# A graph layer on one core: TensorE waits for the gathered rows by a small product, one-hots in pairs, two more groups taken by hand

## The chip, the core and the metric

The kernel runs on one core of a Trainium2 chip. A core has TensorE (PE in the profile; PEld is its loading of weights), VectorE (DVE), ScalarE (ACT), GpSimd (POOL) and SyncE (SP), each with a queue of its own that it works through in order; instructions of different queues are ordered by semaphores. DMA queues are fed by SyncE and GpSimd. The metric is the device time of one launch in microseconds, here the median of three runs.

## The reference, cut to what matters

x has 12,500 nodes of 128 features; there are 400,000 edges, sorted by their destination, each with 32 features of its own.

```python
h = relu(layernorm(x))
m = relu(concat(h[src], h[dst], edge_attr) @ w1 + b1) @ w2 + b2      # per edge
agg = segment_sum(m, dst, num_segments=12500)                        # per node
gi, gh = agg @ w_ih + b_ih, h @ w_hh + b_hh                          # a GRU cell
r, z = sigmoid(gi_r + gh_r), sigmoid(gi_z + gh_z)
n = tanh(gi_n + r * gh_n)
return x + (1 - z) * n + z * h
```

## The kernel before, in words

**Once per node.** The setup normalises x, keeps h transposed in SBUF (`hT_all`), and writes A = h @ w1[0:128] to memory, a row of 128 floats for each node. B = h @ w1[128:256] + b1 is made batch by batch. The product with w2 is moved behind the sum over edges, so an edge needs only relu(A[src] + B[dst] + edge_attr @ w1[256:288]).

**Groups.** The edges are cut into 3125 tiles of 128 and these into NP = 391 groups of 8 tiles (the first has 5). A group's destinations fall into two windows of 32 nodes. For group k and its two halves (units u = 2k and 2k + 1) this is done:

- The rows A[src] are fetched into a buffer `G[k]` (128 edges by 8 tiles by 128 features). As a rule GpSimd does it, by 8 indirect DMAs, one for each tile (`gather`, line 156). There are 11 buffers. The first nine groups (RAW) fetch rows of x instead, and normalise and multiply them.
- `pre` (L673): TensorE multiplies the matrix `L` (one-hots of the destinations and the edges' features, made by VectorE at L575) with `RW` (the window's rows of B, and w1's last rows) into PSUM.
- `add` (L701): in the unit of the second half VectorE adds `G[k]` to the product and takes the relu, for the whole group in one instruction, into one of two buffers `RB`.
- `onehot` (L623): VectorE compares the destinations (`dloc`) with a row of 0 to 31 and writes eight 128 by 32 one-hots into one of six buffers `OH`. The row of numbers lies in columns 256 to 287 of both PSUM banks of sums (`SEGB`); the bank is read that is not open at the time.
- `seg` (L719, L724): TensorE multiplies RB with the one-hots and sums in one of the two banks, which is used for two groups (k // 2 picks it). A product of zeros (L719) opens a bank. `take` (L733) copies the sums of two groups out, in the last quarter of the unit after.

**Groups by hand.** GpSimd doesn't fetch for all groups. 27 are taken by VectorE and 28 by ScalarE, which copy the columns of `hT_all` that the 1024 sources name into `HE` (L960 on ScalarE, one column each; L967 on VectorE, two columns packed into one instruction, and a copy L972 after 128 columns); the numbers are loaded into registers at L945, 16 at a time on ScalarE and 32 on VectorE. TensorE then multiplies `HE` by w1a (L684), adding to the same PSUM, and ScalarE takes the relu (L710) instead of VectorE's add. Two groups are fetched by SyncE, row by row. `SPREAD` says how many groups each takes; they are spread evenly over the 391, and each engine's jobs follow each other without a break: `run_jobs` gives a job's steps out over the four quarters of its units.

**Order.** Everything is written out in Python and compiled in that order; nothing reorders it. In unit u the loop calls `gathers` (asks for the gathers whose buffer is free by program order), a quarter of the hand steps, then `stages(u)`: one-hots for group u // 2 + 3 (odd u), `pre` for unit u + 3, `add` for unit u + 2; then two more quarters of hand steps, `seg(u)`, and in the last quarter `take` and a step of the node work. The node work (`node`, a GRU cell for 512 nodes, some 14 groups each) is cut into steps of one unit.

**Waits.** The framework sets a wait wherever an instruction needs what another engine or a DMA has done, also where TensorE writes into a PSUM bank that another engine reads, whatever the columns. An instruction holds one wait; more stand in event-semaphore instructions of two waits each ahead of it on the same queue. So an `add` of a gathered group has four event semaphores ahead of it, for the eight gathers (each has a semaphore of eight that take turns) and one for TensorE.

Of the kernel before, what the change touches and what calls it, by code (L numbers as in the profile page):

```python
# [9 lines left out]
F32 = mybir.dt.float32  # L10
# [19 lines left out]
V = 32  # L30
# [14 lines left out]
RAW = 9  # L45
# [7 lines left out]
PIECE = 128  # L53
STEP = {"act": 4, "dve": 8, "sp": 4}
ROW = 4 * D
SPREAD = {"dve": 27, "act": 28, "sp": 2}
START = {"dve": 14, "act": 4, "sp": 24}
NR = 12672

# [4 lines left out]
def tile_gnn(ctx: ExitStack, tc: tile.TileContext, x, src, srcT, dstT, dstP, eaT, eaP, w1, b1, w2T, b2,  # L64
             wih, bih, whh, bhh, out):
    nc = tc.nc
    ctx.enter_context(tc.manual_schedule())
    const = ctx.enter_context(tc.tile_pool(name="const", bufs=1))
# [12 lines left out]
    def tiles(k):  # L81
        return (0 if k == 0 else SUP0 + (k - 1) * PAIR, SUP0 + k * PAIR)
# [57 lines left out]
    G = {}  # L140
# [7 lines left out]
    def gather(k):  # L148
        if k >= NP or k in mode:
            return  # L150
        G[k] = gp.tile([128, GRP, 2, D], F32, name="G")
        table = x if k < RAW else A
        for u in (2 * k, 2 * k + 1):
            for t, j, a in unit_tiles(u):
                c, i = divmod(t, CH)
                nc.gpsimd.indirect_dma_start(  # L156
                    out=G[k][:, j, a, :], out_offset=None, in_=table,
                    in_offset=bass.IndirectOffsetOnAxis(ap=src_i[c][:, i:i + 1], axis=0))

    for k in range(RAW):  # L160
        gather(k)
# [2 lines left out]
    RB = [const.tile([128, PAIR, D + 4], F32, name=f"RB{i}") for i in range(2)]  # L164
    for r in RB:
        nc.vector.memset(r[:, :, D:], 1.0)
    OHB = [const.tile([128, GRP, 2, V], F32, name=f"OH{i}") for i in range(6)]
    nc.vector.memset(OHB[0], 0.0)


# [433 lines left out]
                                  "(p f) -> p f", p=V))  # L604

    def onehot(k):
        if k >= NP:
            return
        t0, t1 = tiles(k)
        OH[k] = OHB[k % len(OHB)]  # L610
        row = SEGB[((k - 3) // 2 + 1) % 2][:, 256:256 + V]
        for a in range(2) if k == 0 else (None,):
            if a is None:
                o, s = OH[k].rearrange("p j a v -> p a j v"), slice(t0, t1)
                d = dloc[:, s].rearrange("p (a j) -> p a j", a=2)[:, :, :, None]
                shape = [128, 2, GRP, V]
                i = row[:, None, None, :]
            else:
                e = min(t1, (a + 1) * GRP)
                o, d = OH[k][:, :e - a * GRP, a, :], dloc[:, a * GRP:e, None]  # L620
                shape = [128, e - a * GRP, V]
                i = row[:, None, :]
            nc.vector.tensor_tensor(o, d.to_broadcast(shape), i.to_broadcast(shape),  # L623
                                    op=ALU.is_equal)

    def unit(u):
        k, h = divmod(u, 2)
# [59 lines left out]
    def add(u):  # L687
# [15 lines left out]
        if h == 1:  # L703
            PP.pop(k)
            G.pop(k, None)

    def relu(u):
        if u in RT:
            o, p = RT.pop(u)
            nc.scalar.activation(o, p, AF.Relu)  # L710
# [4 lines left out]
    def seg(u):  # L715
        k, h = divmod(u, 2)
        p = SEGB[(k // 2) % 2]
        if h == 0 and k % 2 == 0:
            nc.tensor.matmul(p[:, :D + 1], zrow[:, :128], zrow[:, :D + 1], start=True, stop=False)  # L719
        l = unit_tiles(u)  # L720
        rest = l if h else l + unit_tiles(u + 1)
        for i, (t, j, a) in enumerate(l):
            r0 = 2 * V * (k % 2) + V * a
            nc.tensor.matmul(p[r0:r0 + V, :D + 1], OH[k][:, j, a, :],  # L724
                             RB[k % 2][:, 2 * j + a, :D + 1], start=False,
                             stop=all(b != a for _, _, b in rest[i + 1:]))

# [206 lines left out]
    def one_by_one(m, k):  # L934
# [8 lines left out]
        for e0 in range(0, PAIR * 128, LOAD[m]):  # L943
# [4 lines left out]
            if m == "sp":  # L948
                for i, v in enumerate(vals):
                    e = e0 + i  # L950
                    a, j = divmod(e // 128, GRP)
                    nc.sync.dma_start(rows[e % 128:e % 128 + 1, j, a, :],
                                      A_bytes[bass.ds(v, ROW)].rearrange("(o f) -> o f", o=1))
                    if i % STEP[m] == STEP[m] - 1:
                        yield
                continue
# [64 lines left out]
    def stages(u):  # L1021
        if u + 7 >= 0:
            raw_stats(u + 7)
        if u + 6 >= 0:
            raw_fin(u + 6)
            raw_h(u + 6)
        if u % 2 == 0:
            onehot_T(u // 2 + 3)
        elif u > -7:
            onehot(u // 2 + 3)  # L1030
        if u + 4 >= 0:
            raw_turn(u + 4)
        if u + 3 >= 0:
            pre(u + 3)
        if u + 2 >= 0:
            add(u + 2)
            relu(u + 2)
# [232 lines left out]
```

## Time and profile before

| | us |
|---|---|
| median of three runs (3400.22 to 3402.1) | 3400.61 |
| the profiled execution | 3403.76 |
| its span, first to last instruction | 3401.8 |
| TensorE busy | 2417.4 (71%) |
| VectorE busy | 2225.1 (65%) |
| ScalarE busy | 3079.4 (91%) |
| GpSimd busy | 2566.1 (75%) |
| mean granted clock of TensorE | 0.796 |

A row by source line reads: line, engine, operation, what it writes from what it reads, shape, count, then the busy time and the mean of one in ns, then the engine's idle time just before these instructions and what ended most of it. Where two instructions overlap on an engine, the mean is longer than busy time by count. "Issue" as the end of idle time means that the profile shows nothing that was waited for: register loads, event semaphores and dispatch are the sequencer's and not counted as busy. A row of the waits reads: who waited, for whom, total, times, longest. A row of the timeline: start, duration, engine, line and operation, count, and in brackets the idle time before it. A row of the windows: the stretch and its length, then for PE, PEld, DVE, ACT and POOL the busy time with the number of instructions, the granted clock, and the DMA engines' share and GB/s. A row of one source line gives the shortest, median and longest duration in ns and the first and last start; a q behind the engine means its sequencer.

### The profile page before, as it was taken

Reading aid. Unit: us, or ns where it says so; the run is one execution under the profiler, and the core shown is the slowest. Engines: PE = TensorE matmul, PEld = TensorE weight load, DVE = VectorE, ACT = ScalarE, POOL = GpSimd, SP = SyncE. Lnnn points to the kernel's source line nnn. Section 1 sums busy time; section 2 is a strip of 40 time slices with the busy share of each in tenths; the row PEclk is TensorE's granted clock in tenths of the full one; section 3 lists DMA queues with packets and bytes.
Section 4 is the critical chain, followed back from the end, with each engine's and each line's share of the span. In section 5 each row is a group of like instructions: output and inputs, shape, how many; then the busy total and the mean of one; then the engine's idle time right before and its main releaser. Section 6 shows DMA issues by size and latency. Waiting matters only on the chain. (4 is left out here: it accounts for less than half of the span.)

```text
span 3401.8 us, 88642 instructions
## 1 busy us (share of the span) xinstructions
PE 2417.4 (71%) x13113; PEld 1563.7 (46%) x13113; DVE 2225.1 (65%) x16468; ACT 3079.4 (91%) x29057; POOL 2566.1 (75%) x2678
## 2 busy tenths in 40 slices
PE   7567777777677767776777667676677767766767
PEld 7444444444445444544444444444444434444445
DVE  8556666666676666666666666666666666666665
ACT  7699999999999998999899988988988898898984
POOL 7777777777777777777777777777777777777776
PEclk9777887887887778777877877788777778777878
DMA  6434444434443333343434433443433334343332
GB/s 213 106 88 93 97 100 99 101 94 100 102 98 94 98 99 95 95 101 97 98 93 99 98 94 93 96 96 93 98 93 92 95 94 99 92 97 96 92 92 73
DMA packets 191316, 335.44 MB, mean 99 GB/s; under 512 B 66753, under 2 KB 112384, under 8 KB 190729
## 3 DMA queue, kind: packets, MB, share of 16 engines
q0 software_dynamic: 85408, 175.09, 23.0%
q1 hardware_dynamic: 105177, 154.58, 16.4%
q14 instruction: 478, 3.92, 0.4%
q8 instruction: 109, 1.79, 0.2%
q10 hardware_dynamic: 144, 0.07, 0.0%
HBM read 309.24 MB, written 20.24 MB: 97 GB/s over the span
## 5 line engine op out<-in xcount | busy, mean ns | idle before, releaser
L156 POOL DMA_INDIRECT G<-A,src_i x2600 | 2498.9, 961 | 796.2 <-issue 753.7
L960 ACT COPY HE_act<-hT_all 128x4 uint8 x28672 | 2886.8, 189 | 51.4 <-issue 27.0
L967 DVE SCALAR_TENSOR_TENSOR both<-hT_all 128x4 uint16 x13824 | 1173.4, 153 | 988.5 <-issue 980.7
L673 PE MATMUL pre<-RW,L 128*128 128x256 f32 x3128 | 1132.4, 488 | 229.8 <-DVE RB L701 220.6
L673 PEld LDWEIGHTS pre<-RW,L 128*128 128x128 f32 x3128 | 660.6, 236 | 506.1 <-DVE RB L701 234.0
L724 PE MATMUL seg<-RB,OH 128*32 128x129 f32 x6250 | 603.9, 324 | 380.0 <-DVE RB L701 349.7
L724 PEld LDWEIGHTS seg<-RB,OH 128*32 128x32 f32 x6250 | 333.1, 125 | 820.4 <-DVE RB L701 532.7
L701 DVE CUSTOM_DVE_ANT_0 RB<-pre,G 128x1024 f32<-128x1024 f32 (+1 forms) x326 | 394.5, 1210 | 62.7 <-DMA G<-A,src_i 49.2
L575 DVE TENSOR_SCALAR L<-L,node_of 64x512 f32<-64x512 int32 x382 | 186.7, 489 | 9.7 <-DMA L<-in_dstP 9.4
L719 PE MATMUL seg<-zrow 1*128 1x129 bf16 x196 | 45.3, 231 | 164.4 <-DVE OH L623 164.2
L623 DVE TENSOR_TENSOR OH<-dloc,seg 128x256 f32<-128x256 f16 (+1 forms) x392 | 159.5, 407 | 0.5 <-issue 0.5
L750 PE MATMUL nd<-spot,sums 128*128 128x40 f32 x782 | 116.6, 321 | 1.2 <-DVE sums L733 1.2
L750 PEld LDWEIGHTS nd<-spot,sums 128*128 128x128 f32 x782 | 112.4, 231 | 10.5 <-issue 9.0
L710 ACT ACTIVATE RB<-pre 128x1024 f32<-128x1024 f32 x64 | 65.0, 1015 | 52.4 <-PE pre L684 52.4
L809 ACT ACTIVATE gt<-nd 128x512 f32<-128x512 f32 (+2 forms) x28 | 16.4, 585 | 96.5 <-PE nd L803 96.5
L972 DVE COPY HE_dve<-both 128x512 uint8<-128x512 uint8 x216 | 96.6, 447 | 7.4
L684 PEld LDWEIGHTS pre<-w1a,HE_act 128*128 128x128 f32 x448 | 88.4, 245 | 11.6
L684 PEld LDWEIGHTS pre<-w1a,HE_dve 128*128 128x128 f32 x432 | 87.9, 252 | 12.1
L684 PE MATMUL pre<-w1a,HE_act 128*128 128x128 f32 x448 | 86.4, 327 | 0.0
L684 PE MATMUL pre<-w1a,HE_dve 128*128 128x128 f32 x432 | 85.1, 333 | 0.0
L156 POOL DMA_INDIRECT G<-in_x,src_i x69 | 65.9, 954 | 21.8 <-issue 20.7
L233 PE MATMUL nd<-w1b,hT_all 128*128 128x128 f32 x224 | 45.5, 346 | 43.3 <-DVE xb L835 43.3
(177 smaller groups left out, 1383.9 us busy)
## 6 DMA issues: line engine op xcount, KB each, us to landing
L<-in_dstP SPq DMA_DIRECT2D x195, 256.0 KB
L<-in_eaP SPq DMA_DIRECT2D x195, 256.0 KB
G<-A,src_i POOLq DMA_INDIRECT x2600
G_sp<-A SPq DMA_DIRECT2D x2048, 0.5 KB
RW<-B SPq DMA_DIRECT2D x782, 16.0 KB
xb<-in_x SPq DMA_DIRECT2D x26, 256.0 KB
out<-xb SPq DMA_DIRECT2D x26, 256.0 KB
xs<-in_x SPq DMA_DIRECT2D x11, 512.0 KB
```

Of the source, the lines that this page charges most:

```text
L156: nc.gpsimd.indirect_dma_start(out=G[k][:, j, a, :], out_offset=None, in_=table, in_offset=bass.IndirectOffsetOnAxis(ap=src_i[c][:, i:i + ...
L575: nc.vector.tensor_scalar(o, i, node_of[:, k:k + 1], None, op0=ALU.is_equal)
L623: nc.vector.tensor_tensor(o, d.to_broadcast(shape), i.to_broadcast(shape), op=ALU.is_equal)
L673: nc.tensor.matmul(p[:, 2 * i:2 * i + 2, :], Ls[k // QP][:, c0:c0 + 128], RW[k % 4], start=True, stop=not raw)
L684: nc.tensor.matmul(p[:, 2 * i + a, :], cols, w1a, start=False, stop=n + 1 == len(l) or l[n + 1][1] != j)
L701: nc.vector._custom_dve(TENSOR_ADD_SAT, out=o, in0=p, in1=G[k].rearrange("p j a f -> p (j a) f")[:, c, :], s0=float("inf"), s1=0.0)
L710: nc.scalar.activation(o, p, AF.Relu)
L724: nc.tensor.matmul(p[r0:r0 + V, :D + 1], OH[k][:, j, a, :], RB[k % 2][:, 2 * j + a, :D + 1], start=False, stop=all(b != a for _, _, b in r ...
L750: nc.tensor.matmul(p[:, bass.ds(offs[i], V + SHIFT)], sums[:, slot(b, i), :D], spot[:, i % 2, :], start=False, stop=i == len(offs) - 1)
L960: nc.scalar.copy(he[:, e * 4:e * 4 + 4], column(v))
L967: nc.vector.scalar_tensor_tensor(both[:, (e0 % PIECE + i) // 2, :], column(vals[i + 1]), 256.0, column(vals[i]), op0=ALU.mult, op1=ALU.add)
L972: nc.vector.tensor_copy(he[:, p0 * 4:(p0 + PIECE) * 4].rearrange("p (n c b) -> p n c b", c=2, b=4), both.bitcast(U8).rearrange("p n (b c) ...
```

## The change

- `SPREAD`: VectorE takes 28 groups by hand, ScalarE 29; so 16 gathers fewer on GpSimd. Being spread evenly, most hand groups get other numbers.
- `arrived`, new, called in `stages` between the one-hots and `pre`: in an odd unit u, for the group that `add` takes in this unit (if it was gathered and is not the last), TensorE multiplies a column of constants with column 0 of the eight rows of `G[k]` and writes eight numbers into columns 320 to 327 of the sums bank that is not open. Nobody reads them. The gathers of the group are put into a dependency group that this product closes: whoever needs the gathers' data later waits for the product instead. So TensorE has the waits for the gathers, and VectorE's `add` waits for TensorE.
- `onehot` makes the one-hots of two groups in one instruction, in the unit in which it made the even group's; three buffers of 16 one-hots take the place of six of 8. The layout becomes flat, and `seg` reads it accordingly.

```diff
-SPREAD = {"dve": 27, "act": 28, "sp": 2}
+SPREAD = {"dve": 28, "act": 29, "sp": 2}
...
-                nc.gpsimd.indirect_dma_start(
+                fetched = nc.gpsimd.indirect_dma_start(
                     out=G[k][:, j, a, :], out_offset=None, in_=table,
                     in_offset=bass.IndirectOffsetOnAxis(ap=src_i[c][:, i:i + 1], axis=0))
+                if RAW <= k < NP - 1:
+                    tc.add_to_no_dep_group(f"rows{k}", fetched.ins)
...
-    OHB = [const.tile([128, GRP, 2, V], F32, name=f"OH{i}") for i in range(6)]
+    OHB = [const.tile([128, 2 * PAIR, V], F32, name=f"OH{i}") for i in range(3)]
...
     def onehot(k):
-        if k >= NP:
+        if k >= NP or (k % 2 and k > 1):
             return
-        t0, t1 = tiles(k)
-        OH[k] = OHB[k % len(OHB)]
+        o = OHB[(k // 2) % len(OHB)]
         row = SEGB[((k - 3) // 2 + 1) % 2][:, 256:256 + V]
...
+        n = 2 if 1 < k < NP - 1 else 1
+        for i in range(n):
+            OH[k + i] = o[:, PAIR * ((k + i) % 2):PAIR * ((k + i) % 2) + PAIR, :]
+        t0, t1 = tiles(k)[0], tiles(k + n - 1)[1]
+        if k:
+            parts = ((o[:, PAIR * (k % 2):PAIR * (k % 2) + t1 - t0, :], t0, t1),)
...
+        for p, e0, e1 in parts:
+            shape = [128, e1 - e0, V]
+            nc.vector.tensor_tensor(p, dloc[:, e0:e1, None].to_broadcast(shape),
+                                    row[:, None, :].to_broadcast(shape), op=ALU.is_equal)
...
+    def arrived(u):
+        k, h = divmod(u, 2)
+        if 0 < u < NU and h and k < NP - 1 and u not in HE and k not in hand:
+            p = SEGB[((u - 2) // 4 + 1) % 2][0:1, 320:320 + PAIR]
+            i = nc.tensor.matmul(p, eps, G[k].rearrange("p j a f -> p (j a) f")[:, :, 0], start=True, stop=True)
+            tc.declare_fence(i.ins, group=f"rows{k}")
...
-            nc.tensor.matmul(p[r0:r0 + V, :D + 1], OH[k][:, j, a, :],
+            nc.tensor.matmul(p[r0:r0 + V, :D + 1], OH[k][:, a * GRP + j, :],
...
-                    nc.sync.dma_start(rows[e % 128:e % 128 + 1, j, a, :],
+                    fetched = nc.sync.dma_start(rows[e % 128:e % 128 + 1, j, a, :],
                                       A_bytes[bass.ds(v, ROW)].rearrange("(o f) -> o f", o=1))
+                    tc.add_to_no_dep_group(f"rows{k}", fetched.ins)
...
             raw_turn(u + 4)
+        arrived(u + 2)
         if u + 3 >= 0:
             pre(u + 3)
```

More of the change, by code (lines that the diff above doesn't have):

```diff
@@ L606, in onehot @@
     def onehot(k):
-        if k >= NP:
+        if k >= NP or (k % 2 and k > 1):
             return
-        t0, t1 = tiles(k)
-        OH[k] = OHB[k % len(OHB)]
+        o = OHB[(k // 2) % len(OHB)]
         row = SEGB[((k - 3) // 2 + 1) % 2][:, 256:256 + V]
[L612 to L624, printed above, removed]
+        n = 2 if 1 < k < NP - 1 else 1
[4 more added lines that the diff above has]
+            parts = ((o[:, PAIR * (k % 2):PAIR * (k % 2) + t1 - t0, :], t0, t1),)
+        else:
+            parts = tuple((OH[0][:, a * GRP:min(t1, (a + 1) * GRP), :], a * GRP, min(t1, (a + 1) * GRP))
+                          for a in range(2))
+        for p, e0, e1 in parts:
+            shape = [128, e1 - e0, V]
+            nc.vector.tensor_tensor(p, dloc[:, e0:e1, None].to_broadcast(shape),
+                                    row[:, None, :].to_broadcast(shape), op=ALU.is_equal)
     def unit(u):
```

## The prediction

> **What bounds the kernel now.** I read the page first for the busy times, then the windows, then the waits, then the lists by source line, and last the timeline of VectorE. The page's rows, with the groups that the change touches (busy time, mean of one, idle time before):
>
> ```profile
> span 3401.8 us, 88642 instructions
> PE 2417.4 (71%) x13113; PEld 1563.7 (46%) x13113; DVE 2225.1 (65%) x16468; ACT 3079.4 (91%) x29057; POOL 2566.1 (75%) x2678
> L156 POOL DMA_INDIRECT G<-A,src_i x2600 | 2498.9, 961 | 796.2 <-issue 753.7
> L960 ACT COPY HE_act<-hT_all 128x4 uint8 x28672 | 2886.8, 189 | 51.4 <-issue 27.0
> L967 DVE SCALAR_TENSOR_TENSOR both<-hT_all 128x4 uint16 x13824 | 1173.4, 153 | 988.5 <-issue 980.7
> L701 DVE CUSTOM_DVE_ANT_0 RB<-pre,G 128x1024 f32<-128x1024 f32 (+1 forms) x326 | 394.5, 1210 | 62.7 <-DMA G<-A,src_i 49.2
> L623 DVE TENSOR_TENSOR OH<-dloc,seg 128x256 f32<-128x256 f16 (+1 forms) x392 | 159.5, 407 | 0.5 <-issue 0.5
> L972 DVE COPY HE_dve<-both 128x512 uint8<-128x512 uint8 x216 | 96.6, 447 | 7.4
> ```
>
> Shares mislead. GpSimd is busy 75%, but in a window of 300 us it issues 238 gathers (the fifth pair; 1.26 us each), and the list by line and its waits say that this holds throughout:
>
> ```profile
> 2700.00:3000.00 300.00, 216.43 (x1144) 135.86 (x1143) 190.91 (x1437) 269.91 (x2586) 227.78 (x238) 0.78 0.39 95
> L156 POOL DMA_INDIRECT G<-A,src_i x2600: 940/945/1552, 92.3 to 3383.9; - x186
> POOL G L156 <- DVE RB L701: 2.6, 7, 0.7
> ```
>
> The second row gives first and last start: (3383.9 - 92.3)/2599 = 1.266 us a gather, and the third that it lost 2.6 us to full buffers. GpSimd never pauses: it sets the end. But VectorE stands just behind it. Its busy 2225.1 and the 980.7 of "issue" are 3206, and what it waits for others at the add is little:
>
> ```profile
> DVE RB L701 <- DMA G<-A,src_i: 49.2, 31, 3.7
> DVE RB L701 <- PE pre L673: 11.6, 6, 2.9
> L945 DVEq TENSOR_LOAD <-at x864: 2095/2150/3239, 188.2 to 3336.5; - x173
> L701 DVEq EVENT_SEMAPHORE  x1358: 21/50/2846, 201.2 to 3386.5; - x194
> ```
>
> The "issue" time is real work of its sequencer: 864 loads of 32 registers at 2.15 us, one before each 16 two-column copies. So VectorE alone needs about 3403.8 - 61 = 3343 us (profiled time less the two waits), only 61 less than the whole. The timeline shows how a load hides:
>
> ```profile
> 1604.53 0.41 DVE L967 SCALAR_TENSOR_TENSOR both<-hT_all 128x4 uint16 x4 [1.06 <-issue]
> 1604.87 0.28 DVE L733 COPY sums<-seg 128x129 f32<-128x129 f32 x1
> ...
> 1605.36 0.41 DVE L623 TENSOR_TENSOR OH<-dloc,seg 128x256 f32<-128x256 f16 x1
> ...
> 1607.45 1.02 DVE L967 SCALAR_TENSOR_TENSOR both<-hT_all 128x4 uint16 x12 [1.04 <-issue]
> ...
> 1610.21 0.99 DVE L967 SCALAR_TENSOR_TENSOR both<-hT_all 128x4 uint16 x12 [1.05 <-issue]
> 1611.12 0.41 DVE L623 TENSOR_TENSOR OH<-dloc,seg 128x256 f32<-128x256 f16 x1
> 1611.45 1.21 DVE L701 CUSTOM_DVE_ANT_0 RB<-pre,G 128x1024 f32<-128x1024 f32 x1
> ...
> 1612.98 0.43 DVE L972 COPY HE_dve<-both 128x512 uint8<-128x512 uint8 x1
> 1615.20 1.49 DVE L967 SCALAR_TENSOR_TENSOR both<-hT_all 128x4 uint16 x16 [1.80 <-issue]
> ...
> 1618.31 0.96 DVE L967 SCALAR_TENSOR_TENSOR both<-hT_all 128x4 uint16 x12 [1.22 <-issue]
> 1619.20 0.27 DVE L733 COPY sums<-seg 128x129 f32<-128x129 f32 x1
> ...
> 1619.71 0.41 DVE L623 TENSOR_TENSOR OH<-dloc,seg 128x256 f32<-128x256 f16 x1
> 1620.04 1.21 DVE L701 CUSTOM_DVE_ANT_0 RB<-pre,G 128x1024 f32<-128x1024 f32 x1
> 1621.65 1.29 DVE L967 SCALAR_TENSOR_TENSOR both<-hT_all 128x4 uint16 x16 [0.39 <-issue]
> ```
>
> From gap to gap is one load with its 16 copies. With sums and a one-hot that is 2.92 us (1604.53 to 1607.45); with an add besides, 3.34 (1618.31 to 1621.65): the add of 1.21 us costs 0.42, as it runs while the next load does. And one-hot and add stand back to back: nothing lies between them on VectorE.
>
> **The change, part by part.** I sum against the profiled execution's 3403.8 us, which is 3.2 (0.1%) above the median of the runs, 3400.6.
>
> *16 gathers leave GpSimd:* 16 x 1.266 = 20.3 us; if it stays the bound, 3383.5. That a buffer's release now also hangs on a product is at most one more wait on the first gather of a group; the 0.3 us of issue time ahead of a gather (796.2/2600) covers it, and uncovered it is 325 x 0.05 (the median wait instruction of VectorE) = 16 us. SyncE's order stays but for a row of addresses for each of the two groups in the setup, where they are asked for three a turn beside the loads of x; uncovered, one more turn, which no row here prices.
>
> *One group more on VectorE:* (1173.4 + 988.5 + 96.6 + 7.4)/27 = 83.9 us, less two adds of 1.21 that ScalarE's relu replaces: +81.5. This lies on VectorE's path, which has 61 to give. *One group more on ScalarE:* (2886.8 + 51.4)/28 = 104.9, plus two relus of about a microsecond. It has 3401.8 - 3079.4 = 322 us without work, part of it forced by others: room, if barely (a rival below).
>
> *VectorE's waits for gathers go:* 1358 of them at 326 adds, four each. In the period without a piece copy they are most of the 0.42 above, so they are worth up to 0.42; in the period from 1610.21 to 1615.20 there is no gap before the copy and they are worth 0. TensorE takes them, with 324 small products of at most 0.37 us (L541 below): 120 us, covered by its 3401.8 - 2417.4 = 984 us without work, of which 349.7 and 164.2 are the waits below. Behind the product in TensorE's queue stand the next group's pre products and the sums of the group before; VectorE's next add waits for the first, its sums copy for the second. Uncovered, that is the third rival.
>
> *One-hots in pairs:* 392 instructions of 407 ns become 198. One of 512 columns should take what such an instruction takes elsewhere:
>
> ```profile
> L813 DVE TENSOR_TENSOR gt<-gt,misc 128x512 f32<-128x512 f32 x26 | 17.6, 678 | 0.1
> PE seg L724 <- DVE RB L701: 349.7, 159, 9.6
> PE seg L719 <- DVE OH L623: 164.2, 64, 8.5
> L541 PE MATMUL seg<-ident,one 128*1 128x128 f32 x1 | 0.4, 372 | 0.0
> ```
>
> so 2 x 407 - 678 = 136 ns a pair, at most 27 us. All pairs are made in odd units ahead of even groups' adds.
>
> *The new wait.* The third row decides the case. L719 is a product that opens a sums bank; it waits for the one-hot, which only reads the iota columns of that bank. So a product into a bank is held until VectorE has finished reading it. The small product writes the same idle bank as the one-hot just ahead of it reads (row and p take the same index, and the one-hot of group k+2 stands in the unit of group k's add, for even k). For an even group the order becomes: one-hot ends, TensorE's product, VectorE's add, which now waits for that product. Before, nothing stood between the two. The round trip's price, from the end of the program, where four transposes stand between two VectorE instructions:
>
> ```profile
> 3395.05 0.50 DVE gt L900
> ...
> 3395.69 0.66 PE nd L903 x4
> ...
> 3396.37 0.68 DVE xb L904
> ```
>
> From 3395.55 to 3396.37 is 0.82; with one product instead of four at least 0.82 - 0.75 x 0.66 = 0.33, at most 0.16 + 0.372 (L541, one column out) = 0.53. I take 0.4. What stands behind the waiting add: the sequencer's next load. Does it go on?
>
> ```profile
> 2400.95 0.75 DVE L238 TENSOR_TENSOR xb<-nd,b1b 128x384 f32<-128x384 f32 x2 [3.59 <-PE nd L233]
> 2403.21 0.38 DVE L967 SCALAR_TENSOR_TENSOR both<-hT_all 128x4 uint16 x4 [1.52 <-issue]
> ```
>
> It doesn't: L238 waited 3.59 us for TensorE, longer than a load, and still the copies came 2.26 us after its start, a whole load later. An add that waits holds the load too. For an even group in a period like that from 1618.31: one-hot at 1619.71 for 0.68, 0.4 of round trip, add at 1620.79, next copies 2.26 later at 1623.05 instead of 1621.65: +1.4, waits and pairing counted. In a period like that from 1610.21 the copy L972 holds the load anyway: +0.27 longer one-hot, +0.4: +0.67. I take 0.75, near the lower end, since an add early in its period leaves copies to be queued beside it. For an odd group there is no one-hot; the product is held by the sums copy L733 of that bank instead. With sums just ahead (ended 1619.47) the add starts at 1619.87, next copies at 1622.13: +0.48; with a load in between, the product is long done and the group gains its 0.42 and some of the one-hot, about -0.45 (ends: -0.75 and +0.48). I take -0.2, as the two cases are about even and the gain has the larger end.
>
> The Trainium skill's page "Perfetto Trace Analysis", section "DVE / Act Engine Instruction", has it otherwise: a waiting instruction sits in a hardware wait queue and the sequencer goes on to fetch. By that rule the load would run under the wait, and the sum would be the first rival's. The row of L238 disagrees, at 1.52 us of idle time behind a wait of 3.59. The page "VectorE: DVE Perf Modes", section "The DRAIN you can't avoid", measured semaphores as costing nothing extra; by it the waits taken off VectorE would be worth nothing, and the forecast higher by up to 160 x 0.42 = 67 us for the odd groups. The 0.42 of this trace speaks against it.
>
> About 2600/8 = 325 groups are gathered, half even: 160 pairs. The sum on VectorE: 3343 + 81.5 + 160 x 0.75 - 160 x 0.2 = 3343 + 81.5 + 120 - 32 = 3512.5, above GpSimd's 3383.5. VectorE becomes the bound, GpSimd waits for buffers, and gathers land early. Less 3.2: 3509. Ends for VectorE with this wait: 3343 + 81.5 + 160 x (0.67 - 0.75) = 3412, and 3343 + 81.5 + 160 x (1.4 + 0.48) = 3725.
>
> **The rivals.**
>
> *The load isn't held, and GpSimd stays the bound (faster).* Then an even period is what the engine has to do: 16 copies 1.22, one-hot 0.68, 0.4, add 1.13 = 3.43 against 3.34, +0.09; an odd one -0.42. VectorE: 3343 + 81.5 - 160 x 0.33 = 3372, below 3383.5, so 3383.5 - 3.2 = 3380. It decides as soon as VectorE's cost of a pair is below (3383.5 - 3424.5)/160 = -0.26 us. For it: the page named above, and 1358 waits do leave VectorE. Against: L238, and 2.26 us from wait to copies. That the product doesn't wait for the one-hot at all would end here too; the row of L719 speaks against it.
>
> *ScalarE becomes the bound (no change).* If the two other engines fit, ScalarE has 107 us more to do. With all of its 322 us without work kept, that gives 3403.8 + 107 = 3511; with a third of them gone it is no change, 3404 - 3.2 = 3401, which I give as this rival's time.
>
> ```profile
> ACT gt L809 <- PE nd L803: 96.5, 20, 9.5
> ```
>
> That is its largest wait, in the node steps, and it shrinks when ScalarE itself is late.
>
> *TensorE comes late (slower still).* It now stays within a group of VectorE at every gathered group, where it could be ahead. Its work is 2417/391 = 6.2 us a group of 3343/391 = 8.5, but gates and sums come in bursts; one microsecond late at a third of 325 adds gives 3509 + 108 = 3617.
>
> **How the numbers follow.** Forecast 0.52, TensorE late 0.10, GpSimd stays the bound 0.30, ScalarE the bound 0.08. So slower 0.62, same 0.08, faster 0.30; 0.2% either way is what a measurement can tell. The forecast's own range is 3410 to 3620. The range has to take in the faster case, which GpSimd bounds sharply at 3380, and leaves out what lies above 3620: 3379 to 3620.
>
> **What would show it.** Right: 198 one-hots of about 678 ns; no event semaphores of VectorE at the add; idle time of VectorE before the add of about 0.4 us each at every second group, put down to the new product; GpSimd waiting for RB by over 50 us; copies x29696 on ScalarE with more idle time. Wrong: GpSimd still at 1.266 us without pause and VectorE's idle time before the add small (then the first rival), or loads that start before a waiting add does.

## The result, and the profile after

| | before | after |
|---|---|---|
| median, us | 3401.36 (4 runs, 3400.22 to 3403.43) | 3665.87 (4 runs, 3656.15 to 3677.95) |
| the profiled span, us | 3401.8 | 3657.4 |
| mean granted clock of TensorE | 0.796 | 0.793 |

The ratio is 1.0779, with a 95% interval of 1.074 to 1.0817: the change makes the kernel 7.8% slower. The forecast was 3509, +3.2%, with a range to 3620; the side was right and the size was not. The prediction's own ends for VectorE with this wait were 3412 and 3725; 3666 lies in the part of them that the stated range left out.

The page of the kernel after, with the rows that answer to those shown of before. The lines of the code have moved: the add is now L702, the one-hot L624, the copy of the sums L741, the copies by hand L976 (VectorE) and L969 (ScalarE); the small product is L712.

```profile
span 3657.4 us, 91316 instructions
PE 2522.3 (69%) x13793; PEld 1610.0 (44%) x13793; DVE 2276.6 (62%) x16792; ACT 3187.6 (87%) x30083; POOL 2545.8 (70%) x2662
...
L969 ACT COPY HE_act<-hT_all 128x4 uint8 x29696 | 2990.4, 189 | 54.0 <-issue 27.1
L156 POOL DMA_INDIRECT G<-A,src_i x2584 | 2478.4, 959 | 980.0 <-issue 742.7 <-DVE RB L702 201.3 <-DMA G<-A,src_i 22.3
L976 DVE SCALAR_TENSOR_TENSOR both<-hT_all 128x4 uint16 x14336 | 1214.8, 154 | 1118.1 <-issue 1111.2 <-DMA RW<-B 4.3
L702 DVE CUSTOM_DVE_ANT_0 RB<-pre,G 128x1024 f32<-128x1024 f32 x324 | 394.6, 1218 | 125.0 <-PE seg L712 112.5 <-PE seg L732 8.4 <-issue 2.0
L624 DVE TENSOR_TENSOR OH<-dloc,seg 128x512 f32<-128x512 f16 (+1 forms) x198 | 132.1, 668 | 0.1
L712 PE MATMUL seg<-G,eps 128*1 128x8 f32 x644 | 64.6, 175 | 1026.5 <-DVE OH L624 618.2 <-DVE sums L741 347.5 <-DMA G_sp<-A 22.1
```

No engine is busier than before in a way that would explain 256 us of span: VectorE has 51 us more to do, TensorE 105, ScalarE 108, GpSimd 20 less. What has grown is idle time. GpSimd, which lost 2.6 us to full buffers before, loses 201.3; VectorE's idle time before the copies went from 988.5 to 1118.1 and that before the adds from 62.7 to 125.0; TensorE stands still for 1026.5 us in front of a product that takes 64.6. The lists by line show the same at the end of the kernel, the adds of before first, then the kernel after:

```profile
L701 DVE CUSTOM_DVE_ANT_0 RB<-pre,G x326: 692/1212/1226, 201.9 to 3386.6; 128x1024 f32<-128x1024 f32 x162, 128x512 f32<-128x512 f32 x1
```

```profile
L156 POOL DMA_INDIRECT G<-A,src_i x2584: 938/944/1534, 92.2 to 3547.5; - x199
...
L702 DVE CUSTOM_DVE_ANT_0 RB<-pre,G x324: 681/1224/1226, 205.6 to 3638.7; 128x1024 f32<-128x1024 f32 x161, 128x512 f32<-128x512 f32 x1
L702 DVEq EVENT_SEMAPHORE  x50: 21/21/50, 205.4 to 3638.1; - x50
...
L953 DVEq TENSOR_LOAD <-at x896: 2096/2151/3199, 188.9 to 3587.9; - x180
```

Before, the last gather started at 3383.9 and the last add 2.7 us behind it. Now the last add stands 91 us behind the last gather, some ten groups at 9.35 us a group (3657.4/391), which is nearly the 11 buffers: VectorE sets the end. Its 1358 event semaphores at the add are 50.

The waits of the kernel after, by who waited for whom:

```profile
PE seg L712 <- DVE OH L624: 618.2, 139, 10.0
...
PE seg L712 <- DVE sums L741: 352.7, 123, 7.5
...
POOL G L156 <- DVE RB L702: 201.3, 65, 14.0
...
ACT RB L718 <- PE pre L685: 180.3, 41, 12.4
...
DVE RB L702 <- PE seg L712: 112.5, 167, 6.7
```

The product hardly ever waits for gathers (22.1 us, and that for the rows that SyncE fetches); it waits for VectorE's one-hot, at even groups, and for its copy of the sums, at odd ones. How one even group goes is seen in VectorE's timeline of the kernel after:

```profile
1621.71 0.99 DVE L976 SCALAR_TENSOR_TENSOR both<-hT_all 128x4 uint16 x12 [1.79 <-issue]
1622.63 0.67 DVE L624 TENSOR_TENSOR OH<-dloc,seg 128x512 f32<-128x512 f16 x1
1623.60 1.23 DVE L702 CUSTOM_DVE_ANT_0 RB<-pre,G 128x1024 f32<-128x1024 f32 x1 [0.29 <-issue]
1624.74 0.39 DVE L976 SCALAR_TENSOR_TENSOR both<-hT_all 128x4 uint16 x4
1625.83 1.27 DVE L976 SCALAR_TENSOR_TENSOR both<-hT_all 128x4 uint16 x16 [0.70 <-issue]
```

and its loads of registers in the stretch from 1620.8 to 1624.9 are these two, with the first and the last start:

```profile
L953 DVEq TENSOR_LOAD <-at x2: 2111/2117/2123, 1619.5 to 1623.6; - x2
```

One-hot, 0.29 us of round trip, add; and the load for the next sixteen copies starts at 1623.6, with the add, not while the add waits. From the first copy behind one load to the first behind the next this period takes 4.12 us (1621.71 to 1625.83); before, a period with an add and a one-hot took 3.34, and a copy of the sums was in it. The example is no exception: of the periods with 16 copies, one one-hot, one add and nothing else, the trace after has 80 with a median of 4.37 us, the trace before 108 with 3.28.

### The profile page after: what moved, and what is told of

It reads as the page before. It is cut to its first block, busy times and chain, and to the rows that moved or that the text cites. A ratio compares the mean times of both kernels' runs of the same rounds, so it can differ in the third digit from the quotient of the medians.

```text
span 3657.4 us, 91316 instructions
## 1 busy us (share of the span) xinstructions
PE 2522.3 (69%) x13793; PEld 1610.0 (44%) x13793; DVE 2276.6 (62%) x16792; ACT 3187.6 (87%) x30083; POOL 2545.8 (70%) x2662
## 5 line engine op out<-in xcount | busy, mean ns | idle before, releaser
L969 ACT COPY HE_act<-hT_all 128x4 uint8 x29696 | 2990.4, 189 | 54.0 <-issue 27.1
L976 DVE SCALAR_TENSOR_TENSOR both<-hT_all 128x4 uint16 x14336 | 1214.8, 154 | 1118.1 <-issue 1111.2
L674 PE MATMUL pre<-RW,L 128*128 128x256 f32 x3128 | 1194.8, 510 | 11.2 <-DMA RW<-B 9.8
L674 PEld LDWEIGHTS pre<-RW,L 128*128 128x128 f32 x3128 | 689.0, 247 | 226.4 <-issue 137.3
L712 PE MATMUL seg<-G,eps 128*1 128x8 f32 x644 | 64.6, 175 | 1026.5 <-DVE OH L624 618.2
L712 PEld LDWEIGHTS seg<-G,eps 128*1 128x1 f32 x644 | 27.8, 81 | 1140.1 <-DVE OH L624 707.7
L702 DVE CUSTOM_DVE_ANT_0 RB<-pre,G 128x1024 f32<-128x1024 f32 x324 | 394.6, 1218 | 125.0 <-PE seg L712 112.5
L624 DVE TENSOR_TENSOR OH<-dloc,seg 128x512 f32<-128x512 f16 (+1 forms) x198 | 132.1, 668 | 0.1
L758 PEld LDWEIGHTS nd<-spot,sums 128*128 128x128 f32 x782 | 125.5, 254 | 9.8 <-issue 9.5
```

The source lines that it names most:

```text
L624: nc.vector.tensor_tensor(p, dloc[:, e0:e1, None].to_broadcast(shape), row[:, None, :].to_broadcast(shape), op=ALU.is_equal)
L674: nc.tensor.matmul(p[:, 2 * i:2 * i + 2, :], Ls[k // QP][:, c0:c0 + 128], RW[k % 4], start=True, stop=not raw)
L702: nc.vector._custom_dve(TENSOR_ADD_SAT, out=o, in0=p, in1=G[k].rearrange("p j a f -> p (j a) f")[:, c, :], s0=float("inf"), s1=0.0)
L712: i = nc.tensor.matmul(p, eps, G[k].rearrange("p j a f -> p (j a) f")[:, :, 0], start=True, stop=True)
L758: nc.tensor.matmul(p[:, bass.ds(offs[i], V + SHIFT)], sums[:, slot(b, i), :D], spot[:, i % 2, :], start=False, stop=i == len(offs) - 1)
L969: nc.scalar.copy(he[:, e * 4:e * 4 + 4], column(v))
```

## The experiments

Some runs fell on chips on which the kernel before itself took 5655 to 5719 us instead of 3400; they stand together in a part of their own, and no size is taken from them. On the chips of the table the kernel before took 3399 to 3410 us, so small differences between two rows are taken from the ratios. Each ratio is to runs of the kernel before on the same chip.

| kernel | groups by hand (VectorE, ScalarE) | product | one-hots | us | ratio to before (95%) |
|---|---|---|---|---|---|
| before | 27, 28 | none | single | 3401 | 1 |
| after | 28, 29 | sums bank | pairs | 3665.9 | 1.0779 (1.074 to 1.0817) |
| the spread alone | 28, 29 | none | single | 3462.3 | 1.0152 (1.0135 to 1.017) |
| the product alone | 27, 28 | sums bank | single | 3688.2 | 1.0815 (1.0795 to 1.0834) |
| pairs alone | 27, 28 | none | pairs | 3411.8 | 1.0007 (0.9997 to 1.0017) |
| after, old spread | 27, 28 | sums bank | pairs | 3568.4 | 1.0459 (1.0429 to 1.0488) |
| after, product in the group's own bank | 28, 29 | own bank | pairs | 3399.4 | 1.0000 (0.9988 to 1.0013) |
| after, row of numbers in SBUF | 28, 29 | sums bank | pairs | 3527.8 | 1.0361 (1.0338 to 1.0384) |
| own bank, 27 and 29 | 27, 29 | own bank | pairs | 3400.1 | 0.9994 (0.9985 to 1.0003) |

**The spread alone.**

```diff
-SPREAD = {"dve": 27, "act": 28, "sp": 2}
+SPREAD = {"dve": 28, "act": 29, "sp": 2}
```

> Only the spread of the kernel after (VectorE 28, ScalarE 29 groups by hand); no product, one-hots of one group. My theory (VectorE is the bound after, and most of the loss is the small product held by VectorE's reads of the sums banks): VectorE alone needed 3343 before, and a group by hand adds 81.5 by busy and issue time, or about 101 as its 32 loads come to 3.15 us each in the trace after; so 3425 to 3445 us, and GpSimd waits a little for buffers. Rival A (the hand groups cause the loss, on VectorE or ScalarE): near the time after, above 3550. Rival B (GpSimd stays the bound with 16 gathers fewer): 3380.

It took 3462.3, +1.5%: more than my 3445, far from the 3550 of the rival. In its lists by line GpSimd keeps its pace and VectorE falls behind it:

```profile
L156 POOL DMA_INDIRECT G<-A,src_i x2584: 942/947/1503, 92.0 to 3372.4; - x199
...
L701 DVE CUSTOM_DVE_ANT_0 RB<-pre,G x324: 682/1217/1227, 203.6 to 3446.8; 128x1024 f32<-128x1024 f32 x161, 128x512 f32<-128x512 f32 x1
```

The last add starts 74 us behind the last gather: one group more by hand is already more than VectorE has room for, and costs 52 us of time (1.52% of 3401) without any product. On VectorE's own path the group costs twice that: its busy time and its "issue" time before the copies were 2225.1 and 980.7, and are now

```profile
PE 2415.0 (70%) x13145; PEld 1555.0 (45%) x13145; DVE 2267.2 (65%) x16986; ACT 3195.8 (92%) x30083; POOL 2556.9 (74%) x2662
DVE both L967 <- issue: 1045.4, 883, 2.9
```

which is 42.1 and 64.7 more, 106.8 together.

**The product alone.** The hunks of the gathers, of `arrived` and of its call, with single one-hots and the old spread; now a one-hot of the idle bank stands ahead of every add.

> Only the small product and its fence (VectorE 27, ScalarE 28; one-hots of one group). A one-hot of the bank into which the product writes now stands just ahead of every add, not of every second one. My theory: 325 adds each wait for the round trip; by the periods of the trace before that is 0.4 us where a piece copy holds the load, and 1.1 where it doesn't, so 3343 + 325 x 0.75 = 3587, with TensorE late at some adds up to 3650; VectorE's idle time before the add mostly put down to the product, at nearly all 325. Rival A (hand groups cause the loss): 3400 to 3420. Rival B (the product costs as such, by TensorE's time or its waits for gathers): also slower, which the product in another bank tells apart.

3688.2, +8.2%: as slow as the whole change, without its hand groups. The waits of this kernel (product L713, one-hot L625, add L703):

```profile
PE seg L713 <- DVE OH L625: 950.0, 263, 7.8
...
POOL G L156 <- DVE RB L703: 206.5, 81, 10.2
...
DVE RB L703 <- PE seg L713: 168.6, 306, 7.2
```

Nearly every add waits for the product (306 times), and the product for the one-hot. Over the time before that is (3688.2 - 3409.6)/325 = 0.86 us for each group; counted as I counted, from VectorE's need of 3343, it is 1.06. My term for such a group, 0.75, gave 3587, and 3688 lies also above the 3650 that I allowed for a late TensorE.

**Pairs alone.** The one-hots in pairs, nothing else.

> Only the one-hots of two groups in one instruction (VectorE 27, ScalarE 28, no product). My theory: VectorE's need falls by at most 27 us to 3316, GpSimd stays the bound: no change, 3395 to 3405, with VectorE's waits for gathers some 25 us longer. Rival (the pairs bring the loss, as VectorE's one-hot of 0.68 us at every second group comes in the wrong place or TensorE waits for it): above 3450.

3411.8 against 3409.6 on the same chip: no change, as expected. VectorE's wait for gathers at the add (L700) is 65.0 us, where it was 49.2:

```profile
DVE RB L700 <- DMA G<-A,src_i: 65.0, 38, 3.9
```

**The change without its hand groups.** The kernel after with 27 and 28.

> The kernel after with the spread of before (27 and 28 groups by hand): product and pairs. My theory: the time after less a hand group of VectorE, 3666 - 81.5 to 101, so 3565 to 3585; GpSimd still waits for buffers. Rival A (hand groups cause the loss): 3400 to 3440. Rival B (ScalarE became the bound through its 104.9 us more): 3666 - 105 = 3560 or less, with VectorE's waits at the add much shorter than in the kernel after.

3568.4, in the range of my theory. Against the kernel after the two groups more by hand are worth 3665.9 - 3568.4 = 98 us, or 109 by the ratios; the prediction's term for VectorE's group was 81.5. ScalarE as the bound is out: with 29 groups in place, the next kernel is 7% faster than the kernel after.

**The product in the group's own bank.** The small product is written into the half of PSUM that the group's own second `pre` overwrites right behind it. No instruction of VectorE reads that half then; the product is the same, it only stands a unit earlier in TensorE's queue.

```diff
         p = PP[k][:, GRP * h:GRP * h + GRP, :]
+        if h and RAW <= k < NP - 1 and k not in hand:
+            i = nc.tensor.matmul(p[0:1, 0, 0:PAIR], eps, G[k].rearrange("p j a f -> p (j a) f")[:, :, 0],
+                                 start=True, stop=True)
+            tc.declare_fence(i.ins, group=f"rows{k}")
...
-        arrived(u + 2)
```

> The kernel after with the small product in the group's own half of PSUM instead of a sums bank, on a chip where the kernel before takes its 3400 us. My theory (the loss is the product's wait for VectorE's reads of the sums bank and the loads held behind the add): VectorE's wait for the product goes, it needs between 3300 and 3462, GpSimd 3380: 3380 to 3430, 7% faster than the kernel after. Rival (the product costs as such, by TensorE's time or its waits for gathers): 3600 or more.

3399.4: the whole loss is gone, 266 us, with the product, the pairs and both hand groups still there. The product (L672) on the page of this kernel, then its gathers and adds (L706) in the lists by line, then VectorE's timeline in a period like the one shown above:

```profile
L672 PE MATMUL pre<-G,eps 128*1 128x8 f32 x644 | 66.3, 177 | 4.8 <-DMA G<-A,src_i 3.9 <-issue 0.8
```

```profile
L156 POOL DMA_INDIRECT G<-A,src_i x2584: 938/944/1645, 92.0 to 3360.6; - x199
...
L706 DVE CUSTOM_DVE_ANT_0 RB<-pre,G x324: 680/1212/1225, 200.4 to 3378.6; 128x1024 f32<-128x1024 f32 x161, 128x512 f32<-128x512 f32 x1
```

```profile
1619.42 1.32 DVE L973 SCALAR_TENSOR_TENSOR both<-hT_all 128x4 uint16 x16 [1.80 <-issue]
1620.67 0.68 DVE L624 TENSOR_TENSOR OH<-dloc,seg 128x512 f32<-128x512 f16 x1
1621.27 1.21 DVE L706 CUSTOM_DVE_ANT_0 RB<-pre,G 128x1024 f32<-128x1024 f32 x1
1622.40 1.27 DVE L973 SCALAR_TENSOR_TENSOR both<-hT_all 128x4 uint16 x16
```

The same 16 copies, one-hot and add take 2.98 us (1619.42 to 1622.40) where the kernel after took 4.12; over the trace 51 such periods have a median of 3.23 us, against 4.37. TensorE's idle time before the product is 4.8 us where it was 1026.5. So the product's own time and its waits for gathers cost nothing in this place. Two things differ from the kernel after, the bank and the place one unit earlier; that it is the reads by VectorE that cost is told by the waits above and, for the one-hot's read, by the next run, which leaves the place as it is. And the idea of the change is worth something: by the ratios this kernel is 1.5% (52 us) faster than the spread alone, with some 1300 event semaphores at the add fewer on VectorE (1358 before, 50 here):

```profile
L706 DVEq EVENT_SEMAPHORE  x50: 21/21/50, 200.0 to 3378.1; - x50
```

At most 27 us of that can be the pairs.

**The row of numbers in SBUF.** The kernel after, but the one-hot compares with a copy of the row in SBUF. So no one-hot reads the product's bank; the copy of the sums still does.

```diff
+    ROWF = const.tile([128, V], F32, name="ROWF")
...
+    nc.vector.tensor_copy(ROWF, iota)
...
-        row = SEGB[((k - 3) // 2 + 1) % 2][:, 256:256 + V]
+        row = ROWF
```

> The kernel after, with the row of numbers that the one-hot compares against read from SBUF and not from the sums bank. So no one-hot reads the bank into which the small product goes, and it waits for sums copies alone; its place, the pairs and the hand groups stay. My prediction's terms: the even groups' 0.75 us goes, 160 x 0.75 = 120, so 3666 - 120 = 3546; by the whole cost of an even group in the trace after (0.9 us) and TensorE late less often, 3480 to 3520. Rival (the sums copies hold the product as much as the one-hots): 3600 or more. Rival (all the loss is the one-hots' hold): 3400, as with the product in the group's own bank.

3527.8: of the 266 us, the one-hot's reads make 138 (142 by the ratios), 0.89 us for each of 160 even groups if all of it is put to these; 128 are left. So the two rivals are out, as the one-hot's read makes about half of the loss, and the sum of an even group was about right: 3546 was forecast from it. Where the rest is, VectorE's waits say, first of this kernel (add L704, copy of sums L743), then of the one with the product in the own bank:

```profile
DVE both L978 <- issue: 1043.8, 834, 2.8
DVE RB L704 <- PE seg L714: 41.4, 25, 4.0
DVE TOT L771 <- PE nd L760: 33.3, 16, 5.0
DVE xb L241 <- PE nd L236: 22.7, 15, 3.3
...
DVE RB L704 <- PE seg L734: 10.2, 9, 1.3
...
PE seg L714 <- DVE sums L743: 587.1, 133, 9.0
```

```profile
DVE both L973 <- issue: 994.4, 817, 2.8
DVE RB L706 <- PE pre L678: 26.4, 13, 6.1
...
DVE TOT L766 <- PE nd L755: 8.2, 4, 3.2
```

Now 133 products wait 4.4 us each for a copy of the sums. VectorE waits little at the add, 25 more (41.4 + 10.2 - 26.4); but it waits 25 and 23 more for TensorE in the steps of the node work (TOT, and xb, where the own bank has no such wait), which stand behind the held product in TensorE's queue, and has 49 more of "issue" before its copies. Together some 120 of the 128. So TensorE comes late, and its largest wait in front of the product is that for the copy of the sums. That this wait is the cause of the 128 us is argued from these rows; no run takes the copies' hold alone away.

**The version that the runs point to.** The own bank with 27 groups on VectorE and 29 on ScalarE.

> The product in the group's own half of PSUM, one-hots in pairs, 27 and 29 groups by hand: the version that the runs point to. With 28 and 29 groups it took 3399, where the last gather started at 3360.6 and VectorE's last add at 3378.6, so that VectorE, not GpSimd, set the end by a little. With one group less VectorE has 80 to 100 us to give, and GpSimd fetches 8 tiles more than there: 3360.6 + 8 x 1.265 = 3370.7 for the last gather, and 18 to 20 from there to the end, as before the change: 3389 to 3394, 0.2 to 0.35% faster than before. Rival: ScalarE with 29 groups sets the end, or VectorE's waits for TensorE do: 3397 or more.

3400.1, ratio 0.9994 with an interval that holds 1: no gain that can be told, where I expected 3389 to 3394. Its gathers and adds in the lists by line, then the product on its page:

```profile
L156 POOL DMA_INDIRECT G<-A,src_i x2592: 938/944/1543, 92.9 to 3372.9; - x200
...
L706 DVE CUSTOM_DVE_ANT_0 RB<-pre,G x325: 691/1215/1226, 203.3 to 3375.5; 128x1024 f32<-128x1024 f32 x162, 128x512 f32<-128x512 f32 x1
```

```profile
L672 PE MATMUL pre<-G,eps 128*1 128x8 f32 x646 | 66.0, 177 | 255.4 <-DMA G<-A,src_i 253.5 <-issue 1.8
```

In this execution GpSimd is the bound again: the last add stands 2.6 us behind the last gather, and TensorE waits 253.5 us for gathers, which nobody pays. VectorE has room again, but the eight gathers saved are at most 10 us (8 x 1.266), and the profiled execution, at 3395.5, is the fastest of the eleven; in the median nothing is left of them. The time is that of the rival (3397 or more), but neither of its two causes sets the end in the execution that was profiled, and what held the others up is open. I found no version that beats the kernel before by more than the measurement can tell.

**On the chips where the kernel before took 5655 to 5719 us.** The product in the group's own bank, with 28 and 29 groups:

> The kernel after, but the small product is written into the group's own half of PSUM, just ahead of the second half's pre products, which then overwrite it (so it stands one unit earlier in TensorE's queue and waits for no read of a sums bank). My theory (the loss is the wait of the product for VectorE's reads, and the held loads behind it): VectorE's wait for the product goes; it needs 3343 + 81.5 to 101 for the group by hand, less up to 0.42 for the event semaphores at each add of 325 and 27 for pairs, so 3300 to 3445, and GpSimd with 3380 is the other limit: 3380 to 3420, 7% faster than the kernel after. Rival (the product costs as such, by TensorE's time or its waits for gathers): 3600 or more, with idle time of TensorE put down to gathers.

> The kernel after, but the small product goes into the group's own half of PSUM just ahead of the second half's pre products; it waits for no read of a sums bank. By what the single parts measured: VectorE needs 3462 with 28 groups by hand and its waits for gathers (the spread alone); these waits, 1358 event semaphores, go (at most 325 x 0.42 = 136) and the pairs give up to 27. So 3300 to 3462 for VectorE and 3380 for GpSimd: 3380 to 3430, 7% faster than the kernel after and about the time before. Rival (the product costs as such, by TensorE's time or its waits for gathers): 3600 or more.

Ratios to before 1.0072 and 1.0074 there. Then the kernel after with the product ahead of the one-hots in program order, in the same bank:

```diff
+        arrived(u + 2)
         if u % 2 == 0:
             onehot_T(u // 2 + 3)
...
-        arrived(u + 2)
```

> The kernel after, with the product ahead of the pair of one-hots in program order instead of behind it; same bank. Now the one-hot must wait for the product where both use one bank, and the product for nothing of VectorE's but the sums copy. My theory: the product can be done well ahead, when TensorE gets to it before VectorE gets to the one-hot; so part of the 618 us that it waited for one-hots goes, and the even groups cost VectorE what the odd ones do; where TensorE is behind, the one-hot waits in place of the add. Between the time after less 160 x 0.9 = 3520 and the time after, 3666; I expect 3560. Rival (the round trip isn't what costs, the product's place in TensorE's queue is): 3666.

> The kernel after, with the product ahead of the pair of one-hots in program order; the same bank. My theory: the product then waits for no one-hot; where TensorE is ahead the even groups cost VectorE no round trip, and where it is behind, the one-hot waits in place of the add. Between 3666 - 160 x 0.9 = 3520 and 3666; I expect 3560. Rival (the round trip isn't what costs, but the product's place in TensorE's queue): 3666.

> The kernel after, with the product ahead of the pair of one-hots in program order; same bank, same place in TensorE's queue but for that. If the round trip one-hot, product, add is what costs (my theory), the product is now done ahead where TensorE has time, and only where TensorE is late does VectorE wait, at the one-hot: below 3600, and the 618 us that the product waited for one-hots gone. Rival: any writing of the shared bank by TensorE beside VectorE's reads costs the same, as the one-hot now waits for the product: 3640 to 3690, with VectorE's idle time moved from the add to the one-hot.

Ratios 1.0253, 1.0281 and 1.0285. The kernel after didn't run on these chips, so they can't be set against its time. In the trace of the third the product has no wait for a one-hot left, where that of the kernel after shows 618.2 us; it waits for copies of the sums:

```profile
PE seg L712 <- DVE sums L741: 247.1, 48, 16.2
```

The own bank without pairs, and with the old spread:

> The kernel before and the product in the group's own half of PSUM (VectorE 27, ScalarE 28, one-hots of one group): what taking the gathers' waits from VectorE is worth with no round trip. My theory: GpSimd stays the bound at 1.266 us a gather: 3395 to 3410, no change, with VectorE's 1358 event semaphores at the add gone and its need smaller by up to 325 x 0.42 = 136. Rival (the product costs as such): 3500 or more.

> The kernel before and the product in the group's own half of PSUM (27 and 28 groups, one-hots of one group). Beside the kernel with the product alone in the sums bank, 3688, it changes only where the product is written and that it stands a unit earlier. My theory: 3395 to 3420, GpSimd's bound, no change against before. Rival (the product costs as such): 3600 or more.

> The kernel before and the product in the group's own half of PSUM (27 and 28 groups by hand, one-hots of one group). Beside the kernel with the product alone in the sums bank (3688) only the place of the product differs. My theory: 3395 to 3410, GpSimd's bound, with VectorE hardly waiting for TensorE at the add. Rival (the product costs as such): 3500 or more.

Ratios 1.0047, 1.0051 and 1.005. The own bank with pairs and the old spread:

> The product in the group's own half of PSUM, with pairs and the spread of before. My theory: 3395 to 3410, GpSimd's bound; beside the same kernel with 28 and 29 groups it tells whether the two groups more now pay (then that one is 20 us faster) or VectorE's 81.5 to 101 still come through. Rival: above 3500.

Ratio 1.0081. And two kernels told above, the row of numbers in SBUF and the own bank with 27 and 29 groups:

> The kernel after, with the row of numbers that the one-hot compares against read from SBUF and not from the sums bank; the product still goes into that bank, so it waits only for sums copies. My prediction's terms: the even groups' 0.75 us goes, 160 x 0.75 = 120, so 3666 - 120 = 3546; if the even groups' whole cost in the trace after (0.9 us) goes and TensorE is late less often, 3480 to 3520. Rival (the sums copies hold the product as much as the one-hots): 3600 or more. A longer one-hot with both inputs in SBUF would add 198 times the difference.

> The product in the group's own half of PSUM, pairs, and 27 and 29 groups by hand: the version that the runs point to. With 28 and 29 groups it took 3399, where the last gather started at 3360.6 and VectorE's last add 18 us behind it, so VectorE sets its end by a little. With one group less VectorE has some 80 us to give, and GpSimd has 8 gathers more than there: 3360.6 + 8 x 1.266 + some 18 to 20 to the end = 3389 to 3393, 0.2 to 0.3% faster than before. Rival: ScalarE with 29 groups, busy 94% there, sets the end: 3397 or more.

Ratios 1.0092 and 1.0212, where the other chips gave 1.0361 and 0.9994: such ratios don't carry over. So it is left open whether the product ahead of the one-hot would save the even groups, and what the own bank does alone, without pairs and with the old spread.

## Why the prediction was wrong in size

**The bound.** Right: GpSimd, then VectorE just behind it; the change makes VectorE the bound, GpSimd waits for buffers (201 us; I asked for over 50), and gathers land early. That ScalarE becomes the bound was rightly given little: it is busy 94% in the kernel at 3399 and less, 87%, in the kernel after.

**The hand group, 81.5.** Too small. It measures 98 to 109 in time, and 106.8 in VectorE's busy and "issue" time of the spread alone. I took busy and "issue" time of 27 groups and divided; why one more costs more than the average of those was not tried. The spread alone came to +52 where my terms gave 3421, +21: some 30 us of the miss stand here, most of them in the group's price and the rest in VectorE's need before, 3343.

**The new wait, even groups, 0.75.** Right in mechanism, place and nearly in size: the product into the idle bank is held by the one-hot that reads the bank's other columns, 161 of 324 adds stand behind a one-hot, most with about 0.3 us of idle time (58.1 in all, summed over the trace) where I took 0.4, and the held load makes the rest. The period that I had at +1.4 grew by 1.09 (medians 3.28 and 4.37). Taking the one-hot's read away gave 0.89 a group.

**The load behind a waiting instruction.** Right, and the first rival (the load runs on, GpSimd stays the bound) falls with it: the load of the timeline above starts with the add at 1623.6, and the same period is 1.14 us longer than without the wait. None of the 183 adds that waited over 0.15 us had a load of 32 registers start in its wait. The Trainium skill's page "Perfetto Trace Analysis", section "DVE / Act Engine Instruction", by which the sequencer goes on behind a waiting instruction, doesn't describe what these loads of registers do here: 0 of 183.

**Waits taken off VectorE are worth something.** Right, and seen only once the product was free: 52 us by the ratios (give or take 8 by their intervals) between the spread alone and the own bank, of which at least 25 aren't the pairs'. The Trainium skill's page "VectorE: DVE Perf Modes", section "The DRAIN you can't avoid", found a semaphore after each of eight copies free; that is another case than four event semaphores ahead of one add, and no run here repeats it.

**The odd groups, -0.2.** This is the step that failed most: a term that I put as a gain was a loss. By the ratios the product and the pairs cost 1.0779 - 1.0152, 213 us or 1.33 a pair of groups, where I had 0.55; the even group took 0.89 of it, so about 0.44 is left for what I had priced as a gain. Two things were wrong. The first is the two cases that I called about even and the gain that I put at 0.45. Of the periods with 16 copies and an odd group's add, 64 hold a copy of the sums ahead of the add, with a median of 3.56 us, and 33 hold nothing else, with 3.18; before, with a one-hot in them, such periods took 3.28 to 3.30. So the loss of 0.48 was 0.26, but the gain of 0.45 was 0.10. The second is that I had looked at VectorE alone: "with a load in between, the product is long done". Mostly it is: of the 163 adds of odd groups, which have no one-hot ahead of them, all but 22 wait less than 0.15 us. But 18 waits of over 1 us make 63.7 of their 66.9, and they come from TensorE: it stands at the product for 353 us behind the copies of the sums and 618 behind the one-hots, and what is queued there (the next `pre`, the sums, the node work) is late when a burst comes.

**TensorE late.** I gave that a chance of 0.10 beside the forecast's 0.52, as if one of them had to be left out: the forecast put it at nothing, as covered by TensorE's 984 us without work. But that time isn't free where it is needed: TensorE now stands 1026.5 us in front of the product. Both came, and they have one cause, since the wait that costs VectorE its round trip also takes TensorE's lead away. The rival's own time was 3509 + 108 = 3617; with the 30 us from the hand group, 3647, against 3666 measured. That this comes near is partly luck, as the 108 (one microsecond at a third of the adds) was a guess that no row gave.

## What to carry to other kernels

A product that only waits for data should write where no other engine reads or copies at that time: in this kernel the same product cost 266 us in a bank that VectorE reads and nothing that could be measured, a unit earlier, in the bank that its group was about to overwrite. When a wait is moved to another engine, count two things and add them: the round trip at the instruction that now waits for that engine, with the register loads held behind it, and the lead that the other engine loses, as everything queued behind its wait comes late too. And an engine 2% behind the bound has no room for one more job: price that by a run of the job alone before it is joined with other edits.

## What was not expected of the hardware

On three chips every kernel that ran took about two thirds more time, the kernel before too. The same program, with the product in its own bank, first on such a chip, then on another:

```profile
L966 ACT COPY HE_act<-hT_all 128x4 uint8 x29696 | 3260.8, 190 | 2044.5 <-issue 2016.2 <-ACT HE_act L966 0.7 <-DVE bn L202 0.3
```

```profile
L966 ACT COPY HE_act<-hT_all 128x4 uint8 x29696 | 2990.2, 189 | 51.0 <-issue 25.9 <-ACT HE_act L966 0.2
```

One copy takes 190 ns on both, but ScalarE spends 2016 us instead of 26 waiting for nothing that the profile shows, and TensorE's granted clock is 0.67 instead of 0.80. What that idle time is wasn't tried, nor whether it belongs to these chips or to the hours at which they ran.
